# An attention and gated-feed-forward block on one core: the scratch of the ternary weights moves into the output weights' place, the fifth key half is there from the start, weight loads get planned times, and square roots are taken for four token tiles at once

## The chip, the cores and the metric

The kernel runs on one NeuronCore of a Trainium2 chip. The metric is the device time of one execution in microseconds (us). The profile times five engines: PE (TensorE, with its weight loads listed as PEld), DVE (VectorE), ACT (ScalarE), POOL (GpSimd) and SP (SyncE, which here only issues DMAs). DMAs are issued from the SP, ACT and POOL instruction streams.

## The reference, cut to what matters

```python
# x: (2, 1024, 512); 32 heads of 16; all float32
xn = layernorm(x)                                     # no gain, no bias
qkv = xn @ w_qkv.T + b_qkv
scores = q @ k.T / 4 + alibi ; causal mask ; softmax ; @ v
s = attention_out @ w_out.T + b_out
# three "octonion ternary" layers: 8 x 8 blocks of signed copies of a weight
# rounded to scale * {-1, 0, 1}, scale = mean(|W|)
h = silu(gate(xn)) * up(xn)                           # 512 -> 1360, twice
g = silu(down(h))                                     # 1360 -> 512
out = x + s * g
```

## The kernel before, in words

**Tiles.** There are 2 batches of 1024 tokens, so 16 token tiles of 128. Heads are taken in groups of four (8 groups for each batch), queries in halves of 512. One batch, group and query half is a *unit*; there are 32 units. For each unit the program makes two passes over the scores. The first, `max_items` (matmuls of line 501, tiles `s1`), finds the row maxima on DVE (`left` L515, mask add L523, `mx` L529). They are split in two parts (`rm`, L557 and L558), transposed on PE (`pm`, L566), copied by ACT (`mr`, L573) and written into two rows of the query stack by two DMAs from the POOL stream (L575). The second pass, `exp_step` (L617, causal mask L634), computes the scores again with the maximum subtracted by the matmul itself; ACT takes the exponential (L639) into a tile `p`, and PE multiplies by the values (`po`, L653). The result is copied (`posb`, L663), transposed (`pt`, L673), divided by the row sum (`o`, L681) and stored to DRAM (`att`, L688).

**Stacks.** Query and key halves of 512 columns live in rings: four `q_stack` tiles and five `k_stack` tiles. `pqk` matmuls (L430) give a query or key chunk; ACT and DVE write its two parts into `st` (L445, L446), SP stores them to DRAM (`sp`, L449), and `fill_k`/`fill_q` load the stacks from there (four DMAs of 128 KB each, L471 and L484, and one of 16 KB, L475).

**The ternary weights.** `load_weight` loads one of `w_g`, `w_u`, `w_d` (340 KB and a swapped copy). `ternary_sum` (DVE, `wsum`, L277), `ternary_total` (PE, `tot`, L283, and DVE) and `ternary_signs` (DVE, L295 and L296, with a scratch `q`) turn it into signs. `keep_signs` (L299) stores the signs of gate and up to DRAM. The down signs are spread out by `expand_down` (ACT, `m_d`, L310, 32 instructions), transposed by `turn_down` (PE, `ptd`, L324), cast by ACT (`md`, L327 and L334) and stored by DMA (`mw`, L328 and L335). The scratch (`q`, `m_d` and one ALiBi part) is in a pool `tmp` of one buffer. The fifth `k_stack` is allocated late: `end_head` closes that pool after the last `turn_down` and then adds the fifth half, and `try_fill` returns as long as a half that is not there is due:

```python
        if (2 * n + part // 2) % 5 >= len(k_ring):
            return
```

**Token tiles 8 to 15** (batch 1) are normalised inside the attention of batch 0: `normal` (DVE L215 and L217, ACT square root L219, DVE L221 and L223, ACT L224), then PE transposes (`ptx`, L354) and an ACT copy into `xnT` (L355).

**Order.** Every engine runs its instructions in the order of the program. That order comes from a planner in the kernel (`step`, `next_max`, `next_exp`, `next_side`, `next_behind` and others). It keeps model clocks for PE, ACT and DVE (`now`, `run_act`, `run_dve`) and emits at each step the item that its model has ready soonest, by priority. `side` holds projections and output products with due places, `behind` the ternary work and the token tiles 8 to 15, in a fixed order, not before a place `begin`. `known` holds the model times at which a load or a result is there. The order and the waits of the built program can be listed without running it: a waiting instruction names the counter it waits on and the value. The DMAs issued from SP and ACT share eight such counters in turn, and a DMA waits until the one before it on its counter has landed, whichever stream issued that one.

After the last attention unit come the last output projections (`pot` L706, `oT` L713, `pout` L722, `y` L733) and the feed-forward part (L1322, L1356), which is the last quarter of the span.

## Time and profile before

| | |
|---|---|
| median of 3 runs | 1190.75 us (1186.47 to 1191.19) |
| profiled execution | 1189.92 us, its span 1188.1 us |
| PE busy | 1076.6 us (91% of the span) |
| DVE busy | 662.9 us (56%) |
| ACT busy | 506.6 us (43%) |
| POOL busy | 176.9 us (15%) |
| mean granted PE clock | 0.963 |

An engine's row in the page's second part has a digit for each fortieth of the span, about 29.7 us, which is the busy share in tenths; `PEclk` gives the granted clock in tenths in the same way. In a row of a group the mean duration of one instruction follows the busy time, and the idle time of the engine just before these instructions stands behind the second bar, with what ended it. A row of the list of waits has the sum, the number and the longest wait. In a timeline row the brackets at the end hold the idle time before the row and its releaser. In a table of stretches each engine has its busy time and, in brackets, its instructions; then follow the granted clock, the DMA share and GB/s.

### The profile page before, as it was taken

What the parts mean: (1) busy time and instruction counts of PE and PEld (TensorE: products, weight loads), DVE (VectorE), ACT (ScalarE), POOL (GpSimd) and SP (SyncE); (2) the same over time, 40 slices, a digit from 0 to 9 for tenths busy, and PEclk for the clock granted to TensorE, in tenths of its full rate; (3) what the DMA queues carried; (4) which work ended last, traced back from release to release, by engine and by line L of the source; (5) the groups of instructions that cost most, each with busy time, mean ns of one, the idle gap of its engine ahead of it and who ended that gap; (6) DMA issues with size and microseconds to landing.
All of it is one profiled execution on the core that took longest, in us unless ns stands there. A gap on an engine that the chain in (4) does not pass through costs nothing.

```text
span 1188.1 us, 15629 instructions
## 1 busy us (share of the span) xinstructions
PE 1076.6 (91%) x5562; PEld 686.4 (58%) x5562; DVE 662.9 (56%) x1411; ACT 506.6 (43%) x972; POOL 176.9 (15%) x296
## 2 busy tenths in 40 slices
PE   7976988889899999988999998999899999999995
PEld 5643555545555566545566554555545677878784
DVE  4555744677677776865867665777843113131212
ACT  4131657446554535535454352544675223232222
POOL 9100040000010100010000000000001124232322
PEclk9997989999899999998999998989999999999998
DMA  6935564426143634364271636343014113020110
GB/s 214 179 84 171 121 157 129 74 72 109 32 87 82 147 53 73 90 134 92 50 152 34 107 74 141 79 63 55 19 41 149 44 46 106 1 74 33 55 53 35
DMA packets 73740, 104.24 MB, mean 88 GB/s; under 512 B 26992, under 2 KB 31120, under 8 KB 73664
## 3 DMA queue, kind: packets, MB, share of 16 engines
q1 hardware_dynamic: 66336, 87.48, 33.1%
q10 hardware_dynamic: 3552, 9.78, 2.7%
q0 software_dynamic: 3776, 5.98, 2.0%
q8 instruction: 45, 0.74, 0.3%
q14 instruction: 31, 0.25, 0.1%
HBM read 69.58 MB, written 33.10 MB: 86 GB/s over the span
## 4 chain that ended last, share of the span: by engine, by line
PE 72%; DVE 12%; DMA 7%; issue 4%; ACT 4%; POOL 1%; SPq 0%; ACTq 0%; DVEq 0%; POOLq 0%
PE s L501 12%; PE s L617 11%; PE po L653 10%; PE pqk L430 8%; PE pg L1322 6%; PE pu L1322 6%; PE pd L1356 5%; PE pout L722 4%; DVE mx L529 4%; PE pv L388 4%; DVE s L523 2%; PE s L634 2%; DVE left L515 2%; DMA q_stack<-mr 2%; PE pm L566 1%
## 5 line engine op out<-in xcount | busy, mean ns | idle before, releaser
L639 ACT ACTIVATE p<-s 128x512 f32<-128x512 f32 x576 | 303.2, 599 | 214.2 <-PE s L634 133.2
L501 PE MATMUL s<-k_stack,q_stack 126*128 126x512 f32 (+3 forms) x768 | 283.3, 431 | 25.8 <-DVE mx L529 19.6
L617 PE MATMUL s<-q_stack,k_stack 128*128 128x512 f32 (+3 forms) x768 | 226.1, 379 | 15.0 <-DMA q_stack<-mr 8.6
L515 DVE TENSOR_REDUCE left<-s 128x1 f32<-128x512 f32 x256 | 170.0, 686 | 91.1 <-PE s L501 89.1
L529 DVE TENSOR_REDUCE mx<-s 128x1 f32<-128x384 f32 (+3 forms) x352 | 217.9, 636 | 4.8
L501 PEld LDWEIGHTS s<-k_stack,q_stack 126*128 126x128 f32 x768 | 135.4, 196 | 122.6 <-issue 35.1
L617 PEld LDWEIGHTS s<-q_stack,k_stack 128*128 128x128 f32 x768 | 138.9, 197 | 70.8 <-ACT p L639 29.2
L523 DVE TENSOR_TENSOR s<-s,mask 128x128 f32<-128x128 f32 (+2 forms) x352 | 120.7, 355 | 98.9 <-PE s L501 94.5
L653 PE MATMUL po<-p,v 128*32 128x512 f32 (+3 forms) x1536 | 144.0, 493 | 0.1
L430 PE MATMUL pqk<-xnT,wq 128*128 128x512 f32 x256 | 132.9, 623 | 5.5 <-ACT xnT L355 2.8
L1333 DVE SCALAR_TENSOR_TENSOR h<-pu,sc_u,sg 128x512 f32<-128x512 f32 (+1 forms) x44 | 33.0, 751 | 166.4 <-PE pu L1322 160.4
L575 POOL DMA_DIRECT2D q_stack<-mr x64 | 32.0, 504 | 619.6 <-ACT mr L573 588.2
L653 PEld LDWEIGHTS po<-p,v 128*32 128x32 f32 x1536 | 44.1, 109 | 77.8 <-issue 67.1
L1339 POOL TENSOR_TENSOR hs<-h,hs 128x512 fp32r<-128x512 f32 (+1 forms) x44 | 57.7, 1311 | 184.7 <-ACT hs L1338 184.7
L1331 ACT ACTIVATE sg<-pg,sc_g 128x512 f32<-128x512 f32 (+1 forms) x44 | 30.2, 687 | 100.2 <-PE pg L1322 95.3
L388 PE MATMUL pv<-wv,xnT 128*128 128x256 f32 x256 | 70.7, 390 | 2.0 <-DVE v L399 1.7
L430 PEld LDWEIGHTS pqk<-xnT,wq 128*128 128x128 f32 x256 | 47.6, 198 | 33.3 <-issue 23.5
L722 PE MATMUL pout<-wo_sb,oT 128*128 128x512 f32 x128 | 62.6, 605 | 1.0 <-DVE y L733 0.7
L1338 ACT CAST hs<-h 128x512 fp32r<-128x512 f32 (+1 forms) x44 | 27.3, 620 | 75.3 <-DVE h L1333 75.3
L445 ACT ACTIVATE st<-pqk,bqk_sb 128x512 fp32r<-128x512 f32 x32 | 22.1, 690 | 84.8 <-PE pqk L430 72.0
L388 PEld LDWEIGHTS pv<-wv,xnT 128*128 128x128 f32 x256 | 46.7, 194 | 12.5 <-DVE v L399 3.2
L634 PE MATMUL s<-mask,ident 128*128 128x256 bf16 (+1 forms) x320 | 53.4, 258 | 0.0
(154 smaller groups left out, 1081.3 us busy)
## 6 DMA issues: line engine op xcount, KB each, us to landing
sp<-st SPq DMA_DIRECT2D x32, 512.0 KB
q_stack<-sp SPq DMA_DIRECT2D x128, 128.0 KB
k_stack<-sp SPq DMA_DIRECT2D x128, 128.0 KB
wqr<-in_wqk_dram ACTq DMA_DIRECT2D x16, 512.0 KB
xt<-in_x_dram SPq DMA_DIRECT2D x16, 256.0 KB
att<-o SPq DMA_DIRECT2D x32, 128.0 KB
ot<-att SPq DMA_DIRECT2D x16, 256.0 KB
proj<-y SPq DMA_DIRECT2D x16, 256.0 KB
```

The lines of the kernel that those rows point to most:

```text
L388: nc.tensor.matmul(ps[:, 0:256], lhsT=xnT[:, c, b * S + kt * P : b * S + (kt + 1) * P], rhs=wv_tiles[2 * b + hh][:, c, :], start=(c == 0), ...
L430: nc.tensor.matmul(ps, lhsT=wq_tiles[b, gp][:, kt, which, :], rhs=xnT[:, kt, b * S + c * 512 : b * S + (c + 1) * 512], start=(kt == 0), st ...
L501: nc.tensor.matmul(ps[:, j * n : (j + 1) * n], lhsT=q_of(b, g, qc)[0 : NR - 2, first + j, tl * P : (tl + 1) * P], rhs=k_of(b, g, c)[0 : NR ...
L515: nc.vector.tensor_reduce(tiles["left"][:, tl, i : i + 1], ps, AX.X, ALU.max)
L523: nc.vector.tensor_tensor(block, block, mask[:, 384:512].rearrange("p (h n) -> p h n", h=1).to_broadcast([P, count, P]), ALU.add,)
L529: nc.vector.tensor_reduce(tiles["mx"][:, tl, first : first + count], ps, AX.X, ALU.max)
L617: nc.tensor.matmul(ps[:, c0 : c0 + w], lhsT=k_of(b, g, kt // 4)[0:NR, h, kt % 4 * P : (kt % 4 + 1) * P], rhs=q[0:NR, h, 512 - w : 512], st ...
L634: pe(nc.tensor.matmul(out, lhsT=ident16, rhs=rhs, start=False, stop=True))
L639: nc.scalar.activation(p[:, c : c + 512], ps, AF.Exp, scale=0.25)
L653: nc.tensor.matmul(po[32 * i : 32 * i + 32, 512 - w : 512], lhsT=v[:, kt, h * VC : h * VC + 32], rhs=p[:, i * part + c0 : i * part + c0 + ...
L722: nc.tensor.matmul(ps, lhsT=turned[t][:, c, :], rhs=wo_sb[:, c, :], start=(c == 0), stop=(c == KD - 1),)
L1322: nc.tensor.matmul(ps[:fs, :], lhsT=fw[mt][:, n0 + kt, 0:fs], rhs=part[:, kt, :], start=(kt == 0 and n == 0), stop=(kt == KD - 1 and n == 1),)
```

## The change

The scratch moves into a new pool `wop`, in the one buffer that later holds the output weights `wo_sb`; `wo_sb` is allocated there by `load_wo`, after the ternary work. Thus `k_stack` 4 is allocated in the lead-in beside 2 and 3 (`add_ring(early, 2, 3)`), and the test in `try_fill` goes. `w_g` moves from the value tiles' pool into that of the `p` tiles. The load of `w_u` no longer waits for `w_g`'s place: it is planned at model time 25 us, the load of `w_d` at 9 us after the up signs. For token tiles 8 to 15, `normal` is split into `measure`, `root` and `normal`, with one root for four tiles; their loads come four at a time. The first batch's output products get later due places (`u + 8 + 4n` to `u + 12 + 4n`). The `memset` of `eps` goes from POOL to DVE, and the first activation reads `ones`. In `step` the `mask_step` call now stands ahead of its model update.

```diff
-    wo_sb = aw.tile([P, KD, D], F32, name="wo_sb")
-    head = ExitStack()
-    tmp = head.enter_context(tc.tile_pool(name="tmp", bufs=1))
+    wop = ctx.enter_context(tc.tile_pool(name="wop", bufs=1))
+    wo_sb = []
...
+    def measure(t, n):
+        if t % n == 0:
+            moments[t // n * n] = wk.tile([P, n, 2], F32, tag=f"mv{n}", name=f"mv_{t}")
+        mv = moments[t // n * n]
+        st = wk.tile([P, 6], F32, tag="lst", name=f"lst_{t}")
+        nc.vector.bn_stats(st, x_tiles[t])
+        nc.vector.bn_aggr(mv[:, t % n, :], st)
+
+    def root(t, n):
+        mv = moments[t]
+        sd = wk.tile([P, n], F32, tag=f"sd{n}", name=f"sd_{t}")
+        nc.scalar.activation(sd, mv[:, :, 1], AF.Sqrt, bias=eps)
+        rs = wk.tile([P, n], F32, tag=f"rs{n}", name=f"rs_{t}")
+        nc.vector.reciprocal(rs, sd)
+        nb = wk.tile([P, n], F32, tag=f"nb{n}", name=f"nb_{t}")
+        nc.vector.scalar_tensor_tensor(nb, mv[:, :, 0], -1.0, rs, ALU.mult, ALU.mult)
+        moments[t] = rs, nb
...
-        w = vp.tile([P, 8, H8], F32, tag="v", name=f"w_{name}")
+        home, tag = (pp, "p") if name == "g" else (vp, "v")
+        w = home.tile([P, 8, H8], F32, tag=tag, name=f"w_{name}")
...
-        q = tmp.tile([P, HID], F32, tag="m", name=f"q_{name}")
+        q = wop.tile([P, HID], F32, tag="wo", name=f"q_{name}")
...
-            nat[kp] = tmp.tile([P, 8, H8], F32, tag="m", name=f"m_d_{kp}")
+            nat[kp] = wop.tile([P, 8, H8], F32, tag="wo", name=f"m_d_{kp}")
...
-            first, last = (u - 1, u) if b + 1 == B else (u + 3 + 4 * n, u + 9 + 4 * n)
+            first, last = (u - 1, u) if b + 1 == B else (u + 8 + 4 * n, u + 12 + 4 * n)
...
-    def end_head():
-        head.close()
-        add_ring(ctx.enter_context(tc.tile_pool(name="late", bufs=1)), 0, 1)
+    def load_wo():
+        wo_sb.append(wop.tile([P, KD, D], F32, tag="wo", name="wo_sb"))
+        pe(nc.gpsimd.dma_start(out=bo_sb, in_=bo.partition_broadcast(P)))
+        pe(nc.gpsimd.dma_start(out=wo_sb[0], in_=wo.rearrange("(k p) n -> p k n", p=P)))
...
-    quick(lambda: (begin_v(0, 0), compact_wq((0, 1)), add_ring(early, 2, 2)))
+    quick(lambda: (begin_v(0, 0), compact_wq((0, 1)), add_ring(early, 2, 3)))
...
+    known["k", "u"] = 25000
+    load_later(wu, "u")
     weight("g")
     later(lambda: keep_signs(0, "g"))
-    load_later(wu, "u")
     begin[0] = 0.6
     weight("u")
-    later(lambda: keep_signs(1, "u"))
+    later(lambda: keep_signs(1, "u"), lambda: set_known(("k", "d"), max(now[0], known["w", "u"]) + 9000))
     load_later(wd, "d")
...
-        if (2 * n + part // 2) % 5 >= len(k_ring):
-            return
...
+            mask_step(ps, pieces)
             run_pe("B", 0, 55 * len(pieces) + 5)
-            mask_step(ps, pieces)
```

More of the change, by code (lines that the diff above doesn't have):

```diff
@@ L108 @@
     eps = const.tile([P, 1], F32, name="eps")
-    nc.gpsimd.memset(eps, EPS)
+    nc.vector.memset(eps, EPS)
     ones = const.tile([64, P], F32, name="ones")
@@ L187, in load_x @@
         x_tiles[t] = xt
-    warm = wk.tile([P, 1], F32, tag="sd", name="warm")
-    nc.scalar.activation(warm, eps, AF.Sqrt)
+    warm = wk.tile([64, 1], F32, tag="rs1", name="warm")
+    nc.scalar.activation(warm, ones[:, 0:1], AF.Sqrt)
     for t in range(8):
@@ L209, with normal @@
     xn_tiles = {}
-    def normal(t):
-        xt = x_tiles.pop(t)
-        st = wk.tile([P, 6], F32, tag="lst", name=f"lst_{t}")
-        nc.vector.bn_stats(st, xt)
-        mv = wk.tile([P, 2], F32, tag="mv", name=f"mv_{t}")
-        nc.vector.bn_aggr(mv, st)
-        sd = wk.tile([P, 1], F32, tag="sd", name=f"sd_{t}")
-        nc.scalar.activation(sd, mv[:, 1:2], AF.Sqrt, bias=eps)
-        rs = wk.tile([P, 1], F32, tag="rs", name=f"rs_{t}")
-        nc.vector.reciprocal(rs, sd)
-        nb = wk.tile([P, 1], F32, tag="nb", name=f"nb_{t}")
-        nc.vector.scalar_tensor_tensor(nb, mv[:, 0:1], -1.0, rs, ALU.mult, ALU.mult)
-        nc.scalar.activation(xt, xt, AF.Identity, bias=nb, scale=rs)
+    moments = {}
+    def measure(t, n):
[14 more added lines that the diff above has]
+        moments[t] = rs, nb
+    def normal(t, n):
+        rs, nb = moments[t // n * n]
+        i = t % n
+        xt = x_tiles.pop(t)
+        nc.scalar.activation(
+            xt, xt, AF.Identity, bias=nb[:, i : i + 1], scale=rs[:, i : i + 1]
+        )
         xn_tiles[t] = xt
@@ L339, in alibi_parts @@
         for n in range(2):
-            home, tag = (stg, "st") if n else (tmp, "m")
+            home, tag = (stg, "st") if n else (wop, "wo")
             part = home.tile([P, S], F32R, tag=tag, name=f"al_{n}")[0:H, :]
@@ L724, in product @@
                     lhsT=turned[t][:, c, :],
-                    rhs=wo_sb[:, c, :],
+                    rhs=wo_sb[0][:, c, :],
                     start=(c == 0),
@@ L807 @@
                 u - 1,
-                lambda n=n: len(k_ring) == 5
+                lambda n=n: not weights_left()
                 and unit_of(vals, V[0]) >= 8 * (n - 1)
@@ L833, with weights_left @@
     behind = []
+    def weights_left():
+        return "weights" not in known
     def waits_x():
@@ L876, in load_later @@
             lambda: set_known(("l", name), now[0] + 9000),
-            "free",
+            ("k", name),
         )
@@ L901, in spread, with more_tokens @@
         )
-    def more_tokens(ts):
-        for t in ts:
+    def more_tokens(t0):
+        for t in range(t0, t0 + 4):
             later(
-                lambda t=t: normal(t),
-                lambda t=t: set_known(("n", t), run_act(run_dve(now[0], 1100) + 300, 700)),
-                "x",
-            )
+                lambda t=t: measure(t, 4),
+                lambda t=t: set_known(("m", t), run_dve(max(now[0], known["x"]), 900)),
+                "x",
+            )
+            begin[0] += 0.2
+        later(
+            lambda: root(t0, 4),
+            lambda: run_dve(run_act(known["m", t0 + 3], 2800), 350),
+        )
+        for t in range(t0, t0 + 4):
+            begin[0] += 0.3
+            later(
+                lambda t=t: normal(t, 4),
+                lambda t=t: set_known(("n", t), run_act(now[0], 720)),
+            )
             later(lambda t=t: norm_item(t), None, ("n", t), 436, "t")
-    def end_head():
-        head.close()
-        add_ring(ctx.enter_context(tc.tile_pool(name="late", bufs=1)), 0, 1)
+    def load_wo():
+        wo_sb.append(wop.tile([P, KD, D], F32, tag="wo", name="wo_sb"))
+        pe(nc.gpsimd.dma_start(out=bo_sb, in_=bo.partition_broadcast(P)))
+        pe(nc.gpsimd.dma_start(out=wo_sb[0], in_=wo.rearrange("(k p) n -> p k n", p=P)))
     idle = ps_e.tile([P, 512], F32, tag="e", name="idle")
@@ L921 @@
     for t in range(8):
-        normal(t)
+        measure(t, 1)
+        root(t, 1)
+        normal(t, 1)
         if t == 3:
@@ L955 @@
             later(lambda kp=kp, f=f: turn_down(kp, f), None, ("e", kp), 436, "t")
-    later(end_head)
-    later(lambda: [load_x(t, nc.sync) for t in range(8, 12)], lambda: set_known("x", now[0] + 9000))
-    for t in range(8, 16):
-        begin[0] = 3 + (t - 8) * 0.6
-        more_tokens([t])
-        if t < 12:
-            later(lambda t=t: load_x(t + 4, nc.sync))
+    later(lambda: set_known("weights", 0))
+    for t0 in (8, 12):
+        begin[0] = 3 if t0 == 8 else 5.4
+        later(
+            lambda t0=t0: [load_x(t, nc.sync) for t in range(t0, t0 + 4)],
+            lambda: set_known("x", now[0] + 9000),
+        )
+        begin[0] += 0.4
+        more_tokens(t0)
     begin[0] = 10
-    later(lambda: pe(nc.gpsimd.dma_start(out=bo_sb, in_=bo.partition_broadcast(P))))
-    later(lambda: pe(nc.gpsimd.dma_start(out=wo_sb, in_=wo.rearrange("(k p) n -> p k n", p=P))))
+    later(load_wo)
     side = [(d, ok or (lambda: True), it) for d, ok, it in lead_in + side]
@@ L1372, in down @@
             eng = nc.vector if st == 3 else nc.gpsimd
-            eng.tensor_tensor(y, y, wo_sb[:, st, :], ALU.add)
+            eng.tensor_tensor(y, y, wo_sb[0][:, st, :], ALU.add)
             nc.sync.dma_start(out=out[n * P : (n + 1) * P, :], in_=y)
@@ L1383, in load_rest @@
         nc.sync.dma_start(
-            out=wo_sb,
+            out=wo_sb[0],
             in_=x[tb * 512 : (tb + 1) * 512, :].rearrange("(s p) n -> p s n", p=P),
```

## The prediction

> **What bounds the kernel now.** I read the slices first, then the table of stretches, then PE's timeline for its gaps, and for the largest gap the list of waits and the chain. The slices say that PE is the engine to watch, and where it is not full:

> ```profile
> PE   7976988889899999988999998999899999999995
> PEclk9997989999899999998999998989999999999998
> ```

> PE works 1076.6 of 1188.1 us, so all that can be won without less work is 111 us of idle time and the low clock after some gaps. The stretches (columns: length, busy us by engine, granted clock, DMA share, GB/s) show where this idle time lies:

> ```profile
> 83.00:99.00 16.00, 0.00 (x0) 0.00 (x0) 2.47 (x3) 0.69 (x1) 0.00 (x0) 0.58 0.86 251
> 150.00:200.00 50.00, 40.94 (x204) 24.88 (x203) 22.36 (x60) 33.46 (x76) 14.96 (x19) 0.86 0.52 136
> 250.00:300.00 50.00, 41.05 (x247) 24.00 (x245) 33.85 (x78) 29.63 (x52) 3.11 (x11) 0.94 0.41 76
> 600.00:700.00 100.00, 96.54 (x571) 60.08 (x570) 68.18 (x150) 45.24 (x86) 3.99 (x8) 1.00 0.45 92
> ```

> A settled stretch (600 to 700) loses 3.5 us in 100. The start loses 16 us in one piece, 9.1 us from 150 to 200 and 9.0 us from 250 to 300. The change works on these places. For the first, waits on all engines from 80 to 100 us and SP's own from 40 to 130 us:

> ```profile
> PE pt L673 <- DVE st L446: 16.2, 1, 16.2
> DVE wsum_u L277 <- DMA w_u<-in_wu_dram: 13.5, 1, 13.5
> ACT st L445 <- DMA sp<-st: 12.3, 1, 12.3
> SPq L484 <- DMA wqr<-in_wqk_dram: 22.1, 1, 22.1
> ```

> and the chain there (start, us, what):

> ```profile
> 82.03 4.35 DMA wqr<-in_wqk_dram
> 86.46 3.55 DMA signs_dram<-w_g
> 90.18 6.60 DMA w_u<-in_wu_dram
> ...
> 98.30 0.74 DVE st L446
> 99.08 1.11 PE pt L673 x4
> ```

> The reader should see two waits that end close together. PE needs the PSUM bank that `st` reads; on DVE `st` stands behind `wsum_u`, which waits for `w_u`, which waits for `w_g`'s place, so for the store of its signs. But ACT's half of `st` had itself waited until 94.4 us, for the store of an earlier `st` out of the same buffer. SP sent that store only at 87.7 us, since it had stood 22.1 us at a `q_stack` fill for a load of `wqr`. They share no data: they share a counter, and ACT issues that load only after `posb` at 81.5.

> The other gaps are in brackets at the end of these timeline rows:

> ```profile
> 168.26 1.01 PE L566 MATMUL pm<-ident,rm 128*8 128x128 f32 x4 [2.02 <-DVE rm L558]
> 190.56 0.66 PE L354 MATMUL ptx<-ident,xt 128*128 128x128 f32 x4 [3.00 <-ACT xt L224]
> 218.54 0.56 PE L617 MATMUL s<-q_stack,k_stack 128*128 128x512 f32 x1 [3.06 <-DMA q_stack<-mr]
> 255.99 0.51 PE L617 MATMUL s<-q_stack,k_stack 128*128 128x512 f32 x1 [3.00 <-ACT p L639]
> 537.72 1.62 PE L617 MATMUL s<-q_stack,k_stack 128*128 128x512 f32 x3 [3.86 <-DMA q_stack<-mr]
> 737.42 1.11 PE L706 MATMUL pot<-ident,ot 128*128 128x128 f32 x4 [5.28 <-DMA ot<-att]
> ```

> **The change, part by part.** Sums are against the profiled execution (span 1188.1, 1.8 us around it, 1189.9), which is 0.8 us under the median of the runs shown; I carry that as nothing. PE's order in the changed program is row for row the same up to about 135 us, so the first parts can be put on the old times.

> *The stall at 83.* `w_u` gets its own place and is issued behind the eighth `xnT` copy, near 32.6 us, so its DVE wait goes. The next latest is ACT's `st`. In the changed program SP still stands at a `q_stack` fill for `wqr`, then at the signs store for the second half of `wqr`, and ACT still issues `wqr` behind `posb`. So the store goes out at 87.7 as before. It took 6.6 us then, beside signs (0.34 MB), `wv` (0.5 MB) and, from 90.2, `w_u` (0.68 MB), which is now absent. A store at 30.3 us let the next fill go after 3.3 us. I take 4.8: landed 92.5, plus 0.69 ACT, 0.75 DVE and small gaps, so PE resumes at 93.7, not 99.1: **5.4 us** won. Between ends: the old 6.6 us gives 3.2, the 3.3 us gives 6.6. The clock is no help: half clock lasts until 103, about 4 us after the gap, and a stall of 10.9 us keeps that.

> *The price of the early load.* `wsum_u` (1.56 us) now stands on DVE ahead of the second pair of `st` (37.1 us before), and behind it waits PE's first `pv`, for a bank, at 39.6. The first part of `w_u` needs about 4 us by the row of `w_g` (4.0), so 36.7 to 38; `wsum_u` ends by 39.6 and `st` by 40.4: under 1 us lost. On SP three `q_stack` fills and a store now share counters with the three parts of `w_u` and go out 2 to 3 us later; first use is at 46.9. DMA share is 1.0 and over from 36 to 44 and from 46 us on, so a landing near 42 is possible. I take **-1** (0 to -5).

> *The load of `w_d`.* Before, PE lost 1.96 us at 138 and DVE waited from 130. Now ACT issues `w_d` behind `posb` of unit 1 and DVE reaches `wsum_d` some 5 us later, against 6.4 us for the load: **+0.5** (-2 to +2).

> *The fifth half, `tmp` and SP.* Before, SP stood for the fifth half until the last `ptd` and `m_d` (a wait of 7.7 us on `ptd`) and filled it up to 174; unit 4's maxima began only at 191. With no maxima to do, DVE worked 22.4 of 50 us from 150 to 200. Now the fill follows unit 0's `att` store, near 100 us, and unit 4's maxima stand on PE ahead of the first `ptd`. That removes the gaps at 168 (2.02, 0.44), 176 (0.59), 179 (1.17) and most of 190 (3.00): 6.5 us. [...]

> ```profile
> 168.00:174.00 6.00, 5.22 (x19) 3.89 (x20) 0.11 (x1) 3.37 (x9) 5.13 (x7) 0.50 0.20 58
> 256.00:260.00 4.00, 4.00 (x9) 2.50 (x10) 1.21 (x4) 1.88 (x4) 0.00 (x0) 0.57 0.00 0
> ```

> 5.22 us at half clock could be 2.6. The row decides: I add 2.6 us for 168 and 1 us for 190 to 196 (granted near 0.7); by the rule it would be 0 of these. Part: 6.5 + 3.6 = **+10** (4 to 14). On POOL the 1.8 us `memset` moves to where POOL is idle (22.7 us until 66), and `eps` costs DVE 0.1 us in its wait for x: nothing, and at most 0.2 without that cover.

> *What moves into unit 3.* `m_d` (32 x 0.43 = 13.8 us of instruction time, 11.2 of busy time), `md` (6.1 + 1.1) now follow unit 2's `posb` and lie among unit 3's exponentials on ACT, which already has 28 x 0.6 = 17 us there. Three score banks full stop PE's second pass; its cover is unit 4's maxima. ACT worked 33.5 of 50 us there before, so room is left, but not for all: **-4** (0 to -18, all of it exposed).

> *Roots of four.* Table loads fall from 11 to 7. By the row that is 4 x 1.28 = 5.1 us of ACT. [...] The timeline has a load at 187.63 and the root at 188.93, with no second such stretch, so I count 5.1. The small DVE and ACT instructions saved (6 roots of 0.29, 6 of each DVE pair) are cover only. Of the gaps with this cause (256: ACT loaded the table, then waited 3.2 us for moments; and 218 and 264 in part) I take half of 8.6 us plus 1.5 us of clock: **+5** (-1 to +8). Against it: each root now waits for four measures, and the second is followed at once by four `xt` of 0.8 us: near 7 us without exponentials, once.

> *Output products later.* 18 PE rows leave 530 to 720 and come between 720 and 890. No work goes away. They fill DVE-made gaps there (785 to 880: about 8 us) and leave others before (DVE 68 in 96.5 PE). `pot` no longer waits at 737, or waits elsewhere: **+3** (-5 to +8). The 3.86 us at 537 stay: SP stands at the same `ot` fetch for the same kind of `wqr` load, 28.6 us, and the fills burst after it. `mask_step` ahead of its model update emits the same thing: 0. `w_g` in a `p` place leaves two until its store at 90; unit 0's third `p` then waits for `po` of the first, done at 78, before its mask is: 0, else 1 us.

> Sum: 5.4 - 1 + 0.5 + 10 - 4 + 5 + 3 = 18.9. So 1189.9 - 18.9 = **1171**.

> **The rivals.** *The moved work takes back what the fifth half gives* (nothing from that half beyond ACT's load, and the products at 0): 5.4 - 1 + 0.5 = 4.9, so 1185. For it: unit 3 is where ACT now has 17 + 19 us. Against: PE has unit 4's maxima. *More than I count*: all gaps of 150 to 310 above the settled 3.5 in 100 go (25.3 - 5.6 = 20) with the clock after them (about 8), the opening as above and 8 from the products: 1189.9 - 41 = 1149. Against: `q_stack<-mr` takes 6.3 us under DMA load, and that stays. *Slower*: ACT in unit 3. If PE cannot go past the banks while ACT spreads `w_d`, all 18 us are exposed; the banks decide, from the point where unit 4's maxima (two PSUM banks, emptied by DVE at 0.69 each) run out or stand behind the stopped score in PE's order. With the gaps of 168 to 190 made again there (no +10, -18) and the rest as counted but no gain from roots, as they queue behind that work: 5.4 - 1 + 0.5 - 18 + 3 = -10, so 1200. Against: the planner's order alternates the two passes row by row.

> **How the numbers follow.** About 0.5% (6 us) is what a measurement of this kernel can tell from no change, so "same" is 1184.8 to 1196.7. Chances: my forecast 0.58 (alone 1160 to 1182), more 0.11, taken back 0.18 (half each side of 1184.8), slower 0.13. Faster 0.58 + 0.11 + 0.09 = 0.78, same 0.09, slower 0.13. The range reaches down to half of "more" and up over "taken back": 1152 to 1192.

> **What would show it.** Right: the gap near 83 is 9 to 12 us and ends with ACT `st` waiting for `sp<-st`; no wait of `wsum_u` over 2 us; 7 table loads; 150 to 200 with PE over 44 and DVE over 30 of 50 us; no gap over 2 us before `pm` there. Wrong: a gap of 15 us still at 83, a new one at 39 to 47 (`pv` or the first `s`), PE waiting for ACT `p` beside `m_d`, or PE under 95 of 100 us from 500 to 700.

## The result, and the profile after

The changed kernel takes 1178.5 us (median of 4 runs, 1177.6 to 1181.9) against 1189.6 us, a ratio of 0.9915 (0.9886 to 0.9945). A second set of runs, among the experiments below, gave 0.9890 (0.9863 to 0.9917). So 10 to 13 us were won, where the forecast said 18.9. The profiled execution took 1178.3 us with a span of 1176.5. PE worked 1065.0 us of it, 11.6 less than before, with the same matmuls; its mean granted clock rose from 0.963 to 0.974. First the slices, as shown for the kernel before:

```profile
PE   7976978998999999989899996999899999999995
...
PEclk9997989999999999989899998999899999999998
```

The stretches (length, busy us by engine, granted clock, DMA share, GB/s), first the stall and the settled part, then those that changed most:

```profile
84.00:96.40 12.40, 0.10 (x1) 0.00 (x0) 1.27 (x3) 0.69 (x1) 0.00 (x0) 0.66 0.82 260
600.00:700.00 100.00, 96.40 (x580) 58.45 (x579) 72.28 (x157) 47.37 (x91) 3.98 (x8) 1.00 0.36 64
```

```profile
150.00:200.00 50.00, 37.11 (x202) 22.29 (x194) 38.94 (x87) 33.17 (x77) 17.44 (x29) 0.93 0.53 137
200.00:250.00 50.00, 47.91 (x321) 31.27 (x322) 31.17 (x68) 27.73 (x52) 2.03 (x4) 1.00 0.32 54
250.00:300.00 50.00, 46.07 (x234) 25.74 (x235) 30.73 (x74) 26.28 (x45) 1.98 (x4) 1.00 0.56 128
500.00:550.00 50.00, 43.25 (x232) 24.21 (x224) 32.39 (x68) 20.08 (x38) 3.98 (x12) 0.93 0.54 123
550.00:600.00 50.00, 44.30 (x253) 26.19 (x250) 32.13 (x69) 22.07 (x43) 3.99 (x12) 0.93 0.44 99
700.00:750.00 50.00, 39.46 (x187) 22.55 (x191) 29.00 (x60) 18.33 (x35) 1.99 (x4) 0.90 0.52 117
```

Three of these stretches in the kernel before:

```profile
200.00:250.00 50.00, 44.27 (x236) 27.09 (x235) 35.97 (x84) 19.20 (x31) 2.03 (x4) 0.97 0.48 101
500.00:550.00 50.00, 42.99 (x221) 24.51 (x220) 30.60 (x67) 19.81 (x37) 5.03 (x11) 0.90 0.47 96
550.00:600.00 50.00, 48.79 (x288) 27.54 (x286) 37.03 (x78) 25.54 (x49) 4.93 (x14) 1.00 0.40 85
```

The stall at the start has become shorter (its row has 0.1 us of PE work in 12.4). The stretch from 150 to 200 is worse than before (37.1 us of PE work, not 40.9), and DVE is now busy there (38.9, not 22.4). The two stretches after it are better by 3.6 and 5.0 us and run at full clock. From 550 to 600 PE works 44.3 us; in the kernel before it was 48.8.

Times of equal work say it better. The table goes from one unit's `posb` to another's. At units 3, 7 and 15 both kernels have done the same or nearly the same work. At units 25 and 31 they have not: the changed kernel has 48 and 8 matmuls of its later output products still to do there that the kernel before has done, so the times at these two borders cannot be compared, only the idle time and the clock. "Idle" is PE's idle time. "Clock" is half of PE's busy time in the stretches that were granted half clock, an estimate, rather high by these rows: the four `pt` matmuls of a row took 1.12 us at half clock (at 96.45, shown below) and 0.66 us at full clock (at 560.87). Both are added up from the timeline and the clock record of the profiled executions.

| up to `posb` of unit | before: ends at, idle, clock | after: ends at, idle, clock |
|---|---|---|
| 3 | 208.2, 38.0, 8.0 | 210.0, 40.5, 5.4 |
| 7 | 326.9, 16.5, 7.4 | 309.0, 5.9, 0 |
| 15 | 510.0, 6.9, 0 | 493.6, 7.4, 0 |
| 25 | 772.6, 18.1, 6.2 | 751.8, 26.9, 9.0 |
| 31 | 892.3, 11.9, 7.7 | 876.3, 9.9, 2.7 |
| end | 1188.1, 20.3, 0 | 1176.5, 21.0, 0 |

In idle time and clock together, units 4 to 7 won 18.0 us (10.6 idle, 7.4 clock) and units 26 to 31 won 7.0, most of it clock. Units 16 to 25 lost 11.6 (8.8 idle, 2.8 clock). The opening, with the stall in it, came out even by these two and ends 1.8 us later. From unit 15 to the end, where the work is the same again, the changed kernel takes 4.8 us longer (682.9 against 678.1 us). Idle time in total is the same in both (111.7 and 111.6), so that the net gain shows as clock; a second profile of the changed kernel has 3 us less idle time and 3.6 us more clock than the first, so the division between the two is rough. The gaps that matter, in brackets:

```profile
96.45 1.12 PE L690 MATMUL pt<-ident,posb 128*128 128x128 f32 x4 [12.36 <-DVE st L463]
```

```profile
162.63 1.98 PE L518 MATMUL s<-k_stack,q_stack 126*128 126x512 f32 x5 [3.48 <-DVE mx L546]
```

```profile
519.10 1.62 PE L634 MATMUL s<-q_stack,k_stack 128*128 128x512 f32 x3 [3.48 <-DMA q_stack<-mr]
...
560.87 0.66 PE L690 MATMUL pt<-ident,posb 128*128 128x128 f32 x4 [1.80 <-DVE st L463]
...
573.05 1.62 PE L634 MATMUL s<-q_stack,k_stack 128*128 128x512 f32 x3 [1.92 <-DMA q_stack<-mr]
```

```profile
717.02 1.09 PE L723 MATMUL pot<-ident,ot 128*128 128x128 f32 x4 [7.51 <-DMA ot<-att]
```

The last three are in the region that the output products had left: the kernel before has no gap over 0.7 us from 540 to 610, and 5.28 us at its `pot`. The gap at 519 is an old one (3.86 us at 537 before). The opening's gap is explained by the list of waits from 80 to 105 us, and SP's own from 60 to 100:

```profile
PE pt L690 <- DVE st L463: 12.4, 1, 12.4
DVE st L463 <- ACT st L462: 12.3, 2, 11.1
ACT st L462 <- DMA sp<-st: 11.6, 1, 11.6
```

```profile
SPq L501 <- DMA wqr<-in_wqk_dram: 19.8, 1, 19.8
```

PE waits for DVE's `st`, that for ACT's, and that for the store `sp` out of the same buffer, as forecast. `wsum_u` is no longer in it. SP stood 19.8 us at a `q_stack` fill for the load of `wqr`.

### The profile page after: what moved, and what is told of

Same layout as the page of the kernel before. It is cut to its first block, busy times and chain, and to the rows that moved or that the text cites. A ratio compares the mean times of both kernels' runs of the same rounds, so it can differ in the third digit from the quotient of the medians.

```text
span 1176.5 us, 15591 instructions
## 1 busy us (share of the span) xinstructions
PE 1065.0 (91%) x5562; PEld 679.8 (58%) x5562; DVE 661.2 (56%) x1400; ACT 500.2 (43%) x962; POOL 177.1 (15%) x295
## 3 DMA queue, kind: packets, MB, share of 16 engines
q1 hardware_dynamic: 66336, 87.48, 33.5%
## 4 chain that ended last, share of the span: by engine, by line
PE 42%; DVE 5%; issue 3%; DMA 2%; ACT 2%; POOL 1%; SPq 0%; DVEq 0%; POOLq 0%; ACTq 0%
PE pg L1357 6%; PE pu L1357 6%; PE s L518 6%; PE s L634 5%; PE po L670 5%; PE pd L1391 5%; PE pout L739 4%; DVE mx L546 2%; PE pqk L447 2%; DVE s L540 1%; PE s L651 1%; PE pv L405 1%; PE pm L583 1%; DMA out_dram<-y 1%; DVE left L532 1%
## 5 line engine op out<-in xcount | busy, mean ns | idle before, releaser
L518 PE MATMUL s<-k_stack,q_stack 126*128 126x512 f32 (+3 forms) x768 | 277.2, 422 | 25.1 <-DVE mx L546 19.1
L634 PE MATMUL s<-q_stack,k_stack 128*128 128x512 f32 (+3 forms) x768 | 222.8, 374 | 12.5 <-DMA q_stack<-mr 9.9
L540 DVE TENSOR_TENSOR s<-s,mask 128x128 f32<-128x128 f32 (+2 forms) x352 | 121.4, 356 | 100.5 <-PE s L518 96.5
L634 PEld LDWEIGHTS s<-q_stack,k_stack 128*128 128x128 f32 x768 | 134.5, 192 | 70.6 <-ACT p L656 29.6
L462 ACT ACTIVATE st<-pqk,bqk_sb 128x512 fp32r<-128x512 f32 x32 | 22.1, 690 | 73.0 <-PE pqk L447 61.2
L590 ACT CAST mr<-pm 8x512 fp32r<-8x512 f32 x32 | 18.3, 572 | 80.2 <-PE pm L583 71.8
```

The costliest lines, as they stand in the source:

```text
L518: nc.tensor.matmul(ps[:, j * n : (j + 1) * n], lhsT=q_of(b, g, qc)[0 : NR - 2, first + j, tl * P : (tl + 1) * P], rhs=k_of(b, g, c)[0 : NR ...
L540: nc.vector.tensor_tensor(block, block, mask[:, 384:512].rearrange("p (h n) -> p h n", h=1).to_broadcast([P, count, P]), ALU.add,)
L634: nc.tensor.matmul(ps[:, c0 : c0 + w], lhsT=k_of(b, g, kt // 4)[0:NR, h, kt % 4 * P : (kt % 4 + 1) * P], rhs=q[0:NR, h, 512 - w : 512], st ...
```

## The experiments

All ratios are to the kernel before, timed on the same chip in the same rounds. The changed kernel is at 0.9915 and 0.9890; "against the changed kernel" below means the range between the differences to these two.

**One part undone at a time.** First the output products' due places:

```diff
-            first, last = (u - 1, u) if b + 1 == B else (u + 8 + 4 * n, u + 12 + 4 * n)
+            first, last = (u - 1, u) if b + 1 == B else (u + 3 + 4 * n, u + 9 + 4 * n)
```

> The changed kernel with the due places of the first batch's output products as before (u + 3 + 4n to u + 9 + 4n). The forecast's sum: 3 us, 1181.5. Reading of the two traces: the lead at unit 15 (16.4 us) and at unit 31 (16.0 us) is the same, with more idle time from 495 to 750 and less half clock after 770, so 1177 to 1180, and the 7.5 us gap at 717 back at about 5 us near 737 less the lead. Rival: later products cost time, as they leave 560 to 620 with two more windows at half clock: 1173 to 1176.

Measured: 1171.55 us, 0.9831 (0.9808 to 0.9853). The later places, which the forecast credited with 3 us, cost 7 to 10 in this kernel. Of the expectations only the last had the sign, and even that asked for less. Stretches and the first gap:

```profile
550.00:600.00 50.00, 48.19 (x279) 28.34 (x282) 38.12 (x80) 23.55 (x45) 3.93 (x12) 1.00 0.45 108
700.00:750.00 50.00, 45.09 (x240) 25.09 (x239) 31.70 (x65) 20.48 (x38) 1.98 (x4) 0.93 0.51 121
```

```profile
717.71 1.11 PE L723 MATMUL pot<-ident,ot 128*128 128x128 f32 x4 [4.02 <-DMA ot<-att]
```

PE works 48.2 of 50 us from 550 to 600 here, 44.3 in the changed kernel; from 700 to 750 it is 45.1 against 39.5. From unit 15's `posb` to the end this kernel has 46.5 us of idle time, the changed one 57.8. In that region both passes stop for DVE (`pt<-DVE st`) and for `mr` (`q_stack<-mr`), and a product on PE beside them fills the time. With the later places less was there to fill it, and the gaps that the products were to fill later (785 to 880 in the kernel before) gave back about 2 us of idle time. The price is shown by the run; that missing filler makes it is read from these rows, and the POOL versions below put a limit on it.

Next, the fifth half added late:

```diff
-    quick(lambda: (begin_v(0, 0), compact_wq((0, 1)), add_ring(early, 2, 3)))
+    quick(lambda: (begin_v(0, 0), compact_wq((0, 1)), add_ring(early, 2, 2)))
...
-    later(lambda: set_known("weights", 0))
+    later(lambda: (set_known("weights", 0), add_ring(early, 0, 1)))
...
+        if (2 * n + part // 2) % 5 >= len(k_ring):
+            return
```

> The changed kernel with the fifth k half allocated only after the last transpose of the down weights, as before; scratch, roots, loads and due places as in the changed kernel. The forecast gave the fifth half 10 us: 1188.5, with gaps ahead of pm near 168 and 190 as before, so lost from 150 to 200. Reading of the two traces: that stretch did not gain (PE 40.9 before, 37.1 after), but units 4 to 7 did, 18 us of idle time and half clock from 210 to 310; if the fifth half did it, 1188 to 1196 with the loss from 210 to 310. Rival: the roots of four did that; then at most 2 us, 1178 to 1181.

Measured: 1199.7 us, 1.0067 (1.0048 to 1.0087), slower than the kernel before and 18 to 21 us slower than the changed one. The loss is not where either expectation had it alone:

```profile
150.00:200.00 50.00, 35.98 (x173) 21.51 (x177) 18.19 (x38) 30.73 (x76) 16.36 (x27) 0.76 0.53 127
200.00:250.00 50.00, 48.25 (x271) 30.57 (x263) 32.73 (x70) 13.90 (x26) 1.04 (x2) 1.00 0.39 82
250.00:300.00 50.00, 41.15 (x236) 23.68 (x236) 33.67 (x76) 29.40 (x51) 3.99 (x12) 0.93 0.41 103
```

```profile
177.75 1.59 PE L341 MATMUL ptd<-ident,m_d 128*128 128x128 f32 x5 [5.20 <-ACT md L351]
```

From 150 to 200 the clock is 0.76, PE waits 5.2 us for `md`, and from 250 to 300 the idle time of the kernel before is back. The early half is the one large gain of this change. The run overstates it as a share of the change, though: here the down weights come late, as in the changed kernel (`m_d` from 167.5 to 191.5; in the kernel before from 142.2 to 169.6), so the half that waits for their end comes later than it did before.

Tokens 8 to 15 one tile at a time (a root for each tile in place of `root(t0, 4)`, loads of the last four one by one, places 0.6 apart):

```diff
+    def more_tokens(t):
+        later(
+            lambda: (measure(t, 1), root(t, 1), normal(t, 1)),
+            lambda: set_known(("n", t), run_act(run_dve(now[0], 1100) + 300, 700)),
+            "x",
+        )
+        later(lambda: norm_item(t), None, ("n", t), 436, "t")
```

> The changed kernel with tokens 8 to 15 normalised one tile at a time, as before (one root for each tile, loads of the last four one by one, places 0.6 apart); the rest as in the changed kernel. The forecast's sum: 5 us, 1183.5, with 11 table loads. Rival: the roots made the gain from 210 to 310, where the kernel before had its gaps of 2 to 3 us: 10 us or more, 1189 to 1194. Rival: table loads are beside other work: 1178 to 1180, and gaps in 200 to 310 about as in the changed kernel (5.9 us idle).

Measured: 1184.32 us, 0.9936 (0.9914 to 0.9958): 2.5 to 5.5 us against the changed kernel, within reach of nothing and of the forecast's 5. This version has 15 table loads, where the kernel before has 11 and the changed one 7, so it goes further than the old order and can overstate the part. Units 4 to 7 have 4.8 us of idle time here, 5.9 in the changed kernel, so the roots did not make the gain there.

The weight loads as before:

```diff
-        home, tag = (pp, "p") if name == "g" else (vp, "v")
+        home, tag = vp, "v"
...
-    known["k", "u"] = 25000
-    load_later(wu, "u")
     weight("g")
     later(lambda: keep_signs(0, "g"))
+    load_later(wu, "u")
```

> The changed kernel with its weight loads as before: w_g in a place of the value tiles, w_u's load behind the store of w_g's signs, w_d's load as soon as its place is free. Everything else as in the changed kernel (1178.5 us). The forecast's sum (opening 5.4 - 1, w_d 0.5): 1183.4, with a gap near 83 of about 16 us. Reading of the two traces: the gap fell from 16.2 to 12.4 us, but the stretch before unit 0's posb became 1.2 us longer, so only about 2.6 us: 1181, the gap again near 16. Rival: the later load of w_d puts its signs (1.0 and 1.6 us on DVE) among unit 4's maxima, which ends in the 3.48 us gap at 162.6; then taking the timing away gives that back, 3.5 us and about 2 us of half clock, and the kernel is as fast as the changed one or faster, 1176 to 1178.5.

Measured: 1184.58 us, 0.9938 (0.9918 to 0.9959), so 2.7 to 5.7 us against the changed kernel: the forecast's 4.9 for these parts is inside. The gap is back at its old size:

```profile
98.63 1.12 PE L690 MATMUL pt<-ident,posb 128*128 128x128 f32 x4 [16.38 <-DVE st L463]
```

**What the rest of the stall is.** The loads of `wqr` are issued from the POOL stream. In the traces of both kernels POOL's DMAs use eight counters of their own (102 to 109) and none of the eight of SP and ACT (101 and 112 to 118). PE's order stays as it was, row for row.

```diff
-                load_wq((n // NP, n % NP), nc.scalar)
+                load_wq((n // NP, n % NP), nc.gpsimd)
```

> The changed kernel with one word changed: the loads of wqr after the first are issued from the POOL stream and not from ACT's, so they no longer share counters with SP's fills and stores. PE's order is row for row the same. The forecast's reading of the 12.4 us gap at 84 (ACT's st waits for a store that SP cannot send, as it stands at a fill for the counter of a wqr load that ACT issues only behind posb): the gap falls to 0 to 5 us, and most of the 17.1 us of half clock after it goes; 8 to 12 us in all, a ratio of about 0.982 to the kernel before. The same coupling holds the ot fetches: the 7.5 us gap at 717 falls too, then up to 18 us in all (0.976). Rival: the store is held by something else (the DMA queues' load, the signs store); the gap stays 10 us or more and the ratio stays 0.990 to 0.994. Rival: POOL's own issue is late (it stands at the sums before the loads): PE waits for wq in its place, ratio 0.995 or above.

Measured: 1165.41 us, 0.9793 (0.9774 to 0.9812), 11.5 to 14.5 us faster than the changed kernel, and 2.1% faster than the kernel before.

```profile
74.43 0.77 PE L634 MATMUL s<-q_stack,k_stack 128*128 128x512 f32 x1 [5.18 <-DMA q_stack<-mr]
...
89.62 0.65 PE L690 MATMUL pt<-ident,posb 128*128 128x128 f32 x4 [1.14 <-DVE st L463]
```

The 12.36 us have become 1.14: the forecast's reading of the wait is shown. A new gap of 5.18 us stands at 74: POOL issues the load 0.5 us behind `mr`, and `mr` lands at 74.3, 8.1 us after its issue (4.8 in the changed kernel). The half clock that followed the stall for 17.1 us is gone, but another 17.1 us stand at 152 (the last section shows them). The lead over the changed kernel is 6.6 us at unit 3's `posb`, 9.3 at unit 15's and 14.7 at the end, so more than half of it comes after unit 3. SP's later wait of 28.7 us for a `wqr` load, from 473 to 502 in the changed kernel, is gone too. The gap of 3.48 us for `mr` that follows it at 519 has hardly changed (3.04 us at 511), so that wait made little of it. The `pot` gap did not fall (6.77 us at 700), so that part of the expectation was wrong: its fetches are not held by `wqr`. The same word in the kernel before, and in the one with the old due places:

> The kernel before with the one word of wq_pool: loads of wqr after the first from the POOL stream; PE's order row for row that of the kernel before. It asks whether the stall at 83 there had two causes (the w_u chain and the held store) or one. If the counter is the root of both (the store of w_g's signs, for whose end w_u's load waits, was itself sent by SP only at 86.5, behind the held fill), the 16.2 us gap falls to under 5 us although w_u still waits for w_g's place, and 8 to 14 us are won: ratio 0.988 to 0.993. If the w_u chain stands by itself, the gap stays 8 to 14 us and the ratio is 0.994 to 1.0.

> The same one word in the kernel with the old due places of the output products (1171.55 us, ratio 0.9831). By the counter theory 8 to 12 us less at the opening, and the ot gap near 717 (4.0 us there) gone: ratio 0.971 to 0.976, about 1160. By the rival, as without: 0.982 to 0.985.

Measured for the kernel before: 0.9933 (0.9909 to 0.9957), so 8 us won. The gap and the ratio both miss the expected bounds narrowly (5.14 us for "under 5", 0.9933 for 0.993).

```profile
73.00 0.47 PE L617 MATMUL s<-q_stack,k_stack 128*128 128x512 f32 x1 [3.59 <-DMA q_stack<-mr]
...
92.50 0.90 PE L673 MATMUL pt<-ident,posb 128*128 128x128 f32 x3 [5.14 <-DVE st L446]
```

```profile
DVE wsum_u L277 <- DMA w_u<-in_wu_dram: 2.4, 1, 2.4
```

So the gap's two causes form a square: 16.23 us with both, 12.36 without the `w_u` chain (the change), 5.14 without the held store, 1.14 without either. The square mixes two kernels, but the changed kernel with the old weight loads stands at 16.38 us, so the other parts of the change hardly move the gap. The larger cause was the one that the change left alone. It was also the root of most of the other: SP sends the signs at 65.6 us, not 86.5, `w_u`'s load is then held only by its place in ACT's stream (86.2), and `wsum_u` waits 2.4 us, not 13.5.

Measured with the old due places: 0.9792 (0.9773 to 0.9812), 1165.56 us, 4.6 us less than without the word, where 8 to 12 were expected. Together, the due places and this word bring no more than the word alone. In these two kernels the due places differ by nothing that the times show. After unit 15 the profiles of the two pairs differ in idle time by 11.3 us without the word and by 2.6 with it. The word took 4.5 us away from the kernel with the later places and added 4.2 to the one with the old places (among them the `mr` gap near 511, 4.32 us, where 2.96 stood near 520 without the word). So the price of the later places is that of a kernel whose `wqr` loads hold SP; why it goes with the word is not settled.

A further version lets POOL issue the load for the third pair of groups only once `mr` has landed:

```diff
+                if n == 2:
+                    late = wk.tile([P, 1], F32, tag="late", name="late")
+                    nc.gpsimd.tensor_copy(late[96:128], q_of(0, 0, 0)[96:128, 0, 0:1].bitcast(F32))
```

> wq_pool with one small POOL copy ahead of the load of wqr for the third pair of groups; it reads a row of the query stack and so lets POOL issue that load only when the first mr has landed there. In wq_pool the load (1 MB) went out 0.1 us behind mr, and mr then took until 74.4, with PE idle for 5.2 us. If the load made that gap, it falls to under 2.5 us and the load still comes in time for the copies into wq at 91: 2.5 to 4 us won, ratio 0.976 to 0.977. Rival: mr is late for another reason, or the load is now late for wq: gap 4 us or more in one of the two places, ratio 0.979 to 0.982.

> The same with the old due places of the output products (due_pool was at 0.9792). If the gap at 74 goes, ratio 0.975 to 0.977; by the rival 0.979 to 0.982. Between this and wq_pool2 no difference beyond 0.002, as between due_pool and wq_pool.

```profile
72.94 0.47 PE L637 MATMUL s<-q_stack,k_stack 128*128 128x512 f32 x1 [2.92 <-DMA q_stack<-mr]
...
86.89 0.66 PE L693 MATMUL pt<-ident,posb 128*128 128x128 f32 x4 [1.13 <-DVE st L466]
```

The gap fell to 2.92 us, between the two expectations, and unit 0's `posb` came 2.7 us earlier. `mr` still took 5.9 us to land, so the load explains 2.2 of its 8.1 us. The ratios are 0.9799 (0.9776 to 0.9822) and 0.9790 (0.9761 to 0.9820): the expected gain is missing, and nothing can be told from the versions without the wait. The profile of the first has lost 2.8 us again after unit 31.

**When the down weights come.** The old due places, with `w_d`'s load planned 9 us earlier:

```diff
-    ... lambda: set_known(("k", "d"), max(now[0], known["w", "u"]) + 9000))
+    ... lambda: set_known(("k", "d"), max(now[0], known["w", "u"])))
```

> The kernel with the old due places, and w_d's load planned at the end of the up signs and not 9 us after. The signs of w_d (1.0 and 1.6 us on DVE) then come earlier than unit 4's first maxima. If they make the 3.5 us gap at 162 and the half clock after it, 3 to 6 us are won: ratio 0.978 to 0.981. Rival: the planner puts them among other maxima, and the time moves by less than 2 us either way: 0.9815 to 0.985.

Measured: 1181.62 us, 0.9920 (0.9892 to 0.9949): 10 us slower than the same kernel with the planned delay, where a gain or nothing was expected. Three of its runs took 1177.4 to 1177.9 us and three 1185.3 to 1186.6, and the profile is of one of the longer ones. The 3.5 us gap is gone, but there are others:

```profile
132.07 0.79 PE L634 MATMUL s<-q_stack,k_stack 128*128 128x512 f32 x1 [2.68 <-ACT p L656]
...
174.94 0.60 PE L583 MATMUL pm<-ident,rm 128*8 128x128 f32 x4 [1.77 <-ACT md L344]
...
177.50 1.11 PE L341 MATMUL ptd<-ident,m_d 128*128 128x128 f32 x4 [1.73 <-ACT md L351]
...
198.44 0.98 PE L634 MATMUL s<-q_stack,k_stack 128*128 128x512 f32 x2 [2.06 <-ACT p L656]
```

They end with ACT, at `p` or at `md`; `m_d` starts at 151.7 and not at 164.4. This is the wait that the forecast's slower rival named, ACT spreading `w_d` among the exponentials. It does not carry the whole loss: at unit 7's `posb`, with the same work done, this profile is 4.3 us behind, and at unit 15's 10.8; what cost the rest was not found. In the changed kernel the plan put `m_d` from 161.9 to 185.3, and the only gap over 1.1 us up to 200 that ends with ACT is 1.55 us.

**The clock.** Twelve matmuls that nothing reads, in the stall ahead of unit 0's `pt`:

```diff
+        if (b, g, qc) == (0, 0, 0):
+            hold = ps_o.tile([P, 512], F32, tag="po", name="hold")
+            for _ in range(12):
+                pe(nc.tensor.matmul(hold, lhsT=ones, rhs=bv_sb[0:64, :], start=True, stop=True))
```

> The changed kernel with 12 extra matmuls (bv with ones, 128x512, into the free bank of po; nothing reads them) ahead of unit 0's pt, in the idle stretch from 84 to 96.4. They add about 10 us of PE work that ends before the wait does. If the lower clock comes from idle stretches alone, the 17.1 us of half clock from 88 to 105 go, and 3.4 us (half of the busy time in them after the gap) are won: ratio 0.9885 against about 0.9915. If the half clock has another cause, nothing is won: 0.991 to 0.993. If the extra matmuls run past the wait, 1 to 3 us are lost.

Measured: 1181.93 us, 0.9918 (0.9897 to 0.9940): nothing won.

```profile
98.97 0.65 PE L694 MATMUL pt<-ident,posb 128*128 128x128 f32 x4 [1.84 <-DVE st L463]
```

The extra work ended 1.84 us before the wait did, so it did not lengthen the stall, and the half clock after the stall did shrink, from 17.1 us to 6.8. But unit 0's `posb`, which stands ahead of the extra matmuls, came 2.5 us later in this execution, and four other stretches of 3.4 us (at 72, 127, 175 and 284) fell to half clock that had been full. So the half clock of the stall went with PE's idle time there (17.1 us of it with 12.36 us idle, 6.8 with the extra matmuls); a price in time the run does not show.

The last experiment is the changed kernel once more:

> The changed kernel itself, once more. Two questions. First the price of the later output products: it rests on 0.9915 (0.9886 to 0.9945) here against 0.9831 for the old due places; if this run gives 0.989 to 0.993, the 10 us stand; if it gives 0.985 or less, most of them were spread. Second the clock: if half clock follows from how the idle stretches fall in windows of 3.41 us, a second profile of the same program has PE's gaps in the same places (12.4 us at 84, 7 us near 717, 3.5 us near 519 and 162) but some of its short half-clock stretches elsewhere, since the windows need not start at the same point; if the clock follows the program alone, all half-clock stretches recur.

Measured: 1176.38 us, 0.9890 (0.9863 to 0.9917). It narrows the price of the due places to the 7 to 10 us above, with intervals that nearly touch. The gaps over 2 us recur. Those near 2 us do not all recur with the same length or effect:

```profile
521.10 1.22 PE L634 MATMUL s<-q_stack,k_stack 128*128 128x512 f32 x3 [4.52 <-DMA q_stack<-mr]
...
571.35 0.93 PE L634 MATMUL s<-q_stack,k_stack 128*128 128x512 f32 x3 [0.95 <-DMA q_stack<-mr]
```

The 1.92 us at 573 are 0.95 here, and the half clock at 562 and 573 is missing, while 170 and 180 have it. So short half-clock stretches belong to the execution as well as to the program.

## Why the prediction was right, and where not

| term of the sum | forecast | measured |
|---|---|---|
| stall at 83 | +5.4 | the gap fell from 16.23 to 12.36: +3.9 |
| early load of `w_u` | -1 | unit 0's `posb` 1.2 us later (0.6 in the second profile): -0.6 to -1.2 |
| load of `w_d` | +0.5 | `tot_d`'s gap is 0.98 us, not 1.96, but `tot_u` has a new one of 1.70; without the delay 10 us lost |
| fifth half | +10 | 18 to 21 by the experiment |
| `m_d`, `md` in unit 3 | -4 | one gap of 1.55 us; no run isolates it |
| roots of four | +5 | 2.5 to 5.5 |
| output products | +3 | -7 to -10 by the experiment |

The measured column does not add up to the 10 to 13 us of the whole: the parts depend on each other, and each of those measured by a run has an interval of about 3 us on either side. That the total still fell well inside the stated range is in part luck: the fifth half was set 8 to 11 us too low and the output products 10 to 13 too high, and these errors cancel.

*Stall.* The mechanism was right, and the wait that the forecast named is shown by the POOL loads. The mis-sized term is the store: sent at 88.85 (forecast 87.7, the 1.2 us of `posb` in it), it let ACT's `st` start at 94.93, 6.1 us later and not 4.8. The old 6.6, the forecast's other end, was nearer. With `posb` later as well, PE resumed at 96.45 and not at 93.7. Of the signs that were named, "9 to 12 us" was missed by 0.4; "no wait of `wsum_u` over 2 us" was false in the letter: DVE waited 5.7 us, beside which no PE gap stands from 39 to 47. The early load's price fell at 71 instead (1.81 us for `mr`, which landed 4.8 us after its issue; 1.7 in the kernel before, and 1.8 in the changed kernel with the old weight loads).

*Fifth half.* The size was too low (10, at most 14; the experiment has 18 to 21, though it overstates it), the place wrong. The forecast counted the gaps of 150 to 200 and took DVE's idle time there as room. Unit 4's maxima did go there, but beside `w_d`'s signs (1.03 and 1.62 us on DVE) they made DVE the bound, with 3.48 us at 162.6. The signs "DVE over 30" and "no gap over 2 us before `pm`" hold, "PE over 44" fails with 37.1. What was won lies in units 4 to 7, 50 to 150 us later: their idle time is 16.5 us in the kernel before, 5.9 in the changed one and 16.4 with the half added late.

*Output products.* This step failed, with its sign. The forecast said that they fill DVE-made gaps from 785 to 880 "and leave others before", and set the second at less than the first. The forecast's own sign of error came true: PE is under 95 from 500 to 600 (87.5), though it was so in the kernel before (91.8). The products had been filling a region whose gaps end with `st`, `mr` and `ot`: after unit 15 PE is idle for 57.8 us with the later places and 46.5 with the old ones. With the POOL loads the price is not seen (0.9793 and 0.9792), so this account of it is not complete.

*Clock.* The forecast read its 3.6 us with the fifth half from the granted clock in its rows (2.6 is half of the 5.22 us of PE work at 0.50 from 168 to 174), and counted 1.5 with the roots: 5.1 us for the clock. Up to unit 7, where these parts lie, the two profiles of the changed kernel have 10.0 and 4.9 us less than that of the kernel before (over the whole span 12.1 and 8.5). The row was the better basis: no run shows a rule by which the 3.6 us would be 0, and in the profiles of the two kernels all 13 steps of the clock record with a gap of 2 us or more were followed by half clock (last section). The size differs too much between executions to say more.

*The rivals.* Neither "taken back" nor "more" describes it; the total lies midway between the forecast and the first of them (1185), but by other losses. The slower one did not occur; the earlier load of `w_d` shows waits of its kind, and 10 us lost.

## What to carry to other kernels

A wait can be for a counter rather than for data: when the list of waits has one queue standing for a load that it does not need, look which stream issues that load and what that stream stands behind, and issue it elsewhere; here one word was worth more than the whole change. Before filler work is moved, count what PE has left in its old place; here the move cost 7 to 10 us as long as SP was held, and nothing that could be measured without that. When a part's gain is read from idle engines in one stretch, ask which engine becomes the bound there.

## What the runs showed of the hardware

```profile
514.62:518.03 3.41, 1.00 (x4) 0.31 (x2) 1.96 (x5) 0.00 (x0) 0.00 (x0) 1.00 1.10 210
518.03:521.44 3.41, 2.34 (x6) 1.90 (x7) 0.33 (x2) 1.48 (x3) 0.00 (x0) 0.50 0.41 142
521.44:524.86 3.42, 3.42 (x8) 2.00 (x7) 1.62 (x4) 1.03 (x3) 0.00 (x0) 0.50 0.00 0
524.86:528.27 3.41, 3.41 (x15) 1.68 (x17) 2.14 (x6) 3.19 (x8) 0.00 (x0) 1.00 0.02 5
610.19:613.60 3.41, 2.40 (x11) 1.75 (x11) 2.84 (x8) 0.00 (x0) 0.00 (x0) 1.00 0.00 0
613.60:617.01 3.41, 3.41 (x21) 2.70 (x21) 2.88 (x8) 0.57 (x1) 0.01 (x1) 1.00 0.15 38
```

```profile
149.08:152.49 3.41, 1.66 (x5) 0.66 (x4) 3.41 (x11) 0.00 (x0) 0.27 (x2) 1.00 0.76 244
152.49:155.91 3.42, 1.08 (x3) 0.64 (x3) 3.33 (x6) 1.87 (x6) 0.00 (x0) 0.50 0.76 255
155.91:159.32 3.41, 2.92 (x14) 2.63 (x13) 2.58 (x7) 2.03 (x5) 0.79 (x1) 0.50 0.02 5
159.32:162.73 3.41, 2.40 (x10) 1.74 (x10) 1.80 (x5) 2.03 (x7) 1.97 (x4) 0.50 0.52 156
162.73:166.15 3.42, 2.54 (x8) 1.95 (x9) 2.90 (x8) 1.69 (x6) 1.15 (x2) 0.50 0.18 53
166.15:169.56 3.41, 3.41 (x14) 2.80 (x12) 1.67 (x5) 2.45 (x5) 1.43 (x2) 0.50 0.25 77
169.56:172.97 3.41, 2.34 (x9) 1.20 (x7) 3.00 (x8) 3.25 (x11) 1.41 (x3) 1.00 0.43 130
```

In the first fence a step with 1.00 us of PE work (29%) is followed by half clock; the next, with 2.34 us (69%), is followed by half clock again, and one of 3.42 by full clock. The step at full clock with 2.40 us (70%) is followed by full clock. In the profiles of the kernel before and of the changed kernel, from 23 us on, with the steps laid on the changes in the clock record: after a full-clock step with a busy share under 0.4 the next was at half clock in 12 of 12, from 0.4 to 0.5 in 7 of 7, from 0.5 to 0.6 in 1 of 6, from 0.6 to 0.8 in 2 of 53, and above that in none of 557. Of these 22 falls, 7 came after a step whose longest gap within it was under 1.5 us; where that gap was 2 us or more, all 13 steps were followed by half clock. From half clock it came back after none of 23 steps under 0.8, one of 2 from 0.8 to 0.9 and all 19 over 0.9. The second fence shows how long this lasted once, with DVE busy for 3.41 and 3.33 us of its first two steps: a step at 49% is followed by half clock, and PE stays at half clock for five steps, 17 us, though it is busy for 70 to 86% of three of them. The steps begin at other points in other executions: 2.6 us past a multiple of 3.413 us from the span's start in the profile of the changed kernel, 0.3 us in that of the kernel before. A step need not be idle throughout for half clock to follow it: the one ahead of the prediction's 2.02 us gap, 164.18 to 167.59 in the kernel before, has 1.58 us of PE work (46%) and no gap over 1.35 us, and half clock lasts from its end for 6.8 us.
